# Mixture of experts on tiles of two 64-row halves, biases as a product with the gates, and a last tile in two parts

## The chip, the cores and the metric

The kernel runs on one core of one Trainium2 chip. A core has five instruction queues that run at the same time and meet through semaphores: TensorE (PE in the profile; PEld is its weight load), VectorE (DVE), ScalarE (ACT), GpSimd (POOL) and SyncE (SP, which here only issues transfers and loads registers). The metric is the time of one execution on the device, in microseconds (us); lower is better. The kernel before took 1554.63 us, the median of 5 runs (1551.43 to 1561.74).

## What is computed

A stack of four blocks on `x` (16 batches of 112 tokens, 256 features, float32). Each block adds gated cross attention to a context of 375 tokens a batch and then a gated feed-forward part. Layers 0 and 1 have a mixture of eight experts as feed-forward part, with two experts for each token; layer 2 has eight experts with a fixed share of the tokens; layer 3 has a gated unit whose operands are all quantised to 4 bits in blocks of 16.

```python
x = x + tanh(g_xattn[l]) * attention_l(layernorm(x), ctx)      # l = 0..3; layer 1 has a mask
x = x + tanh(g_ffn[l]) * ffn_l(layernorm(x))

# ffn of layer 0 (layer 1: the softmax over the two chosen experts alone)
gates = softmax(x @ gate_w.T + gate_b)
top_gates, top_idx = top_k(gates, 2)
expert_out[e] = x @ expert_w[e].T + expert_b[e]
out = sum over the two chosen experts of top_gate * expert_out

# ffn of layer 3; w_gate and w_up are 704 x 256, w_down is 256 x 704
h = silu(fp4(x) @ fp4(w_gate).T) * (fp4(x) @ fp4(w_up).T)
out = fp4(h) @ fp4(w_down).T
```

The inputs have biases for the experts of both mixtures that are not zero.

## The kernel before

Everything stays in SBUF as far as it fits: `x` as four tiles of four batches (a group `g`, 448 tokens), the transposed context of all batches. PSUM is two pools: `wide` (line 62), three tiles of two banks, and `bank` (line 66), two tiles of one bank. Whoever asks for a fourth wide tile waits until the first has been read.

The order of instructions on PE, ACT, DVE and POOL is written out by hand, in the order of the Python code. Only SP's order is the scheduler's own: it places each transfer and each register load by its estimate of when it can go.

- **Layers 0 to 2, attention.** `unmasked` (L712) writes the order for layers 0 and 2, one batch after the other; `with_mask` (L839) for layer 1, in 64 units of four heads. A unit in layer 1 computes the scores of the next unit on PE (L449), takes them through the mask on DVE (L615), finds maxima (L632), takes exponentials on ACT (L635), turns them on PE (L647, copied at L651), and multiplies with the values (L664). In layers 0 and 2 the scores are computed twice, once for the maxima (L449, L465) and once transposed (L500, with the maxima added by L512) for the exponentials (L521), and weighted at L536.
- **The mixtures run in the gaps.** Between the attention's pieces the hand-written order calls `fill()` (L1256). A call takes one step of each of three lines of generators: `route` (L975), `products` (L1138) and `combine` (L1207). Each line works on one group of one layer at a time, and passes it to the next line. There are eight jobs: layers 0 and 1, four groups each. The mixture of layer 0 so lies beside the end of layer 0's attention and the start of layer 1's; that of layer 1 beside layer 1's and layer 2's.
- **`route`** normalises the group's rows (`xn`), computes gates, chooses two experts for each token (`top2`), and finds for each token and chosen expert a row in a table in DRAM (`rows_in`): each expert has a region of 512 rows, and a token's place in it is its rank among the tokens of that expert (`pp`, a product with a triangle). Eight indirect transfers from POOL (L1101) write the rows there. A small table (L1124 to L1129) gives, for each of 14 tiles of 128 rows, the expert and the first row.
- **`products`** goes through the 14 tiles (`NS`). Each tile reads its expert and its first row from the table into registers of SP (L1148, L1155), loads 128 rows (`xg`), the expert's weights (`w`, 256 KB) and its bias to all partitions (`wb`), multiplies (L1186), transposes the next tile's rows (L1196), and copies both results out of one PSUM tile with one ACT copy (L1198). POOL adds the bias (L1169); the result goes to `rows_out` in DRAM at the tile's row (L1166). A job has 19 steps.
- **`combine`** gathers for each token its two rows (L1216, POOL's queue) and adds them to `x`, each times its gate (L1224).
- **Tail.** The quantised down weights of layer 3 are made in steps beside layer 0's attention (`weights_down`, L1482) and kept in SBUF (`wd`, L1801). `last_block` (L1547) runs attention and feed-forward of layer 3: 14 tiles of 128 tokens, each with gate and up products (L1688), `silu` (L1698), product (L1700), quantisation over several steps (`fp4`, L1403 to L1422), six transpositions (L1712), a copy (L1716), the down product (L1722) and an add (L1732). Their steps are interleaved with the next tiles' steps; the last tile has nothing behind it.

At the start, SP issues the first weights and contexts one after the other, and ACT issues three small loads. The tables' 4992 rows (`ROWS`) are cleared in DRAM four times during layer 0 (L967).

Of the kernel before, what the change touches and what calls it, by code (L numbers as in the profile page):

```python
# [12 lines left out]
F32 = mybir.dt.float32  # L13
I32 = mybir.dt.int32
U32 = mybir.dt.uint32
# [17 lines left out]
WB, XB = 3, 3  # L33
CAP = 512
NS = (2 * GS + E * (P - 1)) // P
ROWS = E * CAP + (NS - 2 * GS // P) * P
# [11 lines left out]
def tile_gated_xattn_stack(ctx: ExitStack, tc: tile.TileContext, a: dict, out: bass.AP):  # L48
# [29 lines left out]
    def load_ctx(b):  # L78
        nc.gpsimd.memset(ctxZ[b][:, :, T:], 0.0)
        nc.sync.dma_start(ctxT[b], a["ctx"][:, :, b * T : (b + 1) * T])  # L80

    w_first = {n: wpool.tile([P, 2, D], F32, tag=n, name=f"w_0_{n}") for n in ("wq", "wk", "wv", "wo")}
    for n in ("wk", 0, "wv", "x", "wq", 1, "wo"):
        if n == "x":
            load_x(0)
        elif n in w_first:
            nc.sync.dma_start(w_first[n], a[f"L0_xattn_{n}"])
        else:
            load_ctx(n)
# [7 lines left out]
    hmask = const.tile([P, 2], F32, tag="hmask", name="hmask")  # L97
    nc.scalar.dma_start(hmask, a["head_mask"])
# [16 lines left out]

    region = ramp(S, E, CAP, "region")[:, None, :].to_broadcast([S, G, E])
    filled = ramp(E, CAP // P, P, "filled")
    slots = ramp(E, NS, 1, "slots")
    slot_rows = ramp(1, NS, P, "slot_rows")
    coef = const.tile([E, 2], F32, tag="coef", name="coef")  # L120
    nc.gpsimd.memset(coef, 1.0)
    graw = const.tile([P, 8], F32, tag="graw", name="graw")
    nc.scalar.dma_start(graw[:, 0:4], a["g_xattn"].partition_broadcast(P))
    nc.scalar.dma_start(graw[:, 4:8], a["g_ffn"].partition_broadcast(P))
# [131 lines left out]
    def attention(pool, layer, w):  # L256
# [455 lines left out]
        def unmasked(nxt, block):  # L712
# [21 lines left out]
            for b in range(B):  # L734
# [44 lines left out]
                if b == 1:  # L779
                    if layer == 0:  # L780
                        prepare()
                        said["side"] = weights_down(wd)
# [145 lines left out]
    def top2(v, nm):  # L928

        picked = []  # L930
        for i in range(2):
            m = small.tile([S, G], F32, tag="tm", name=f"tm_{nm}_{i}", bufs=2)
            nc.vector.tensor_reduce(m, v, AX.X, ALU.max)
            eq = small.tile([S, G, E], F32, tag="teq", name=f"teq_{nm}_{i}", bufs=2)
# [7 lines left out]
            if i == 0:  # L942
                v2 = small.tile([S, G, E], F32, tag="tv", name=f"tv_{nm}", bufs=2)
# [17 lines left out]
    gate_weights = {}  # L961
# [9 lines left out]
    def mixture_weights(layer):  # L971
        L = f"L{layer}_ffn_"
        gate_weights[layer] = load(wpool, L + "gate_w", [P, 2, E], "gw"), load_row(L + "gate_b", "gb", E)

    def route(layer, g, out):  # L975
# [41 lines left out]
        lg = small.tile([S, G, E], F32, tag="lg", name=f"lg_{nm}", bufs=2)  # L1017
# [27 lines left out]
        picked, keep = chosen  # L1045
        keepb = small.tile([S, G * E], BF16, tag="keepb", name=f"keepb_{nm}", bufs=2)
        nc.vector.tensor_copy(keepb, keep.rearrange("s g e -> s (g e)"))
        nc.vector.tensor_scalar(gt, gt, gate[:S, 4 + layer : 5 + layer], None, ALU.mult)
# [31 lines left out]
        over = small.tile([E, CAP // P], F32, tag="over", name=f"over_{nm}", bufs=2)  # L1080
        nc.vector.tensor_scalar(over, filled, cnt, None, ALU.is_lt)
        tiles_of = small.tile([E, 1], F32, tag="ntiles", name=f"ntiles_{nm}", bufs=2)
        nc.vector.tensor_reduce(tiles_of, over, AX.X, ALU.add)
        place = small.tile([S, G, E], F32, tag="place", name=f"place_{nm}", bufs=2)
        nc.vector.tensor_tensor(place, pp[:S, : G * E].rearrange("s (g e) -> s g e", e=E), region, ALU.add)
# [6 lines left out]
        nc.vector.tensor_copy(index, at)  # L1092
        out.update(picks=picks, index=index)
# [14 lines left out]

        copy_out(0, 0)
        yield  # L1110
        copy_out(0, 1)
        yield
        pe = wide(f"pends_{nm}")[:, 0, :]
        nc.tensor.matmul(pe[:E, 0:1], tri8, tiles_of, start=True, stop=True)
        ends = small.tile([E, 1], F32, tag="ends", name=f"ends_{nm}", bufs=2)
        nc.vector.tensor_copy(ends, pe[:E, 0:1])
        behind = small.tile([E, NS], F32, tag="behind", name=f"behind_{nm}", bufs=2)
        nc.vector.tensor_scalar(behind, slots, ends, None, ALU.is_ge)
        nc.vector.tensor_scalar(coef[:, 1:2], tiles_of, -float(P), float(CAP), ALU.mult, ALU.add)
        copy_out(1, 0)  # L1120
        yield
        pt = wide(f"ptab_{nm}")[:, 0, :]
        for i in range(2):
            nc.tensor.matmul(  # L1124
# [769 lines left out]
```

## Time and profile before

| what | value |
|---|---|
| median of 5 runs | 1554.63 us (1551.43 to 1561.74) |
| the profiled execution, its own time | 1555.78 us |
| its span, first to last instruction | 1554.1 us |
| mean granted TensorE clock | 0.973 |
| L1186, products of the mixtures | 118.8 us busy |
| L1196, transpositions of their rows | 40.5 us busy |
| L1198, ACT copies of both | 63.2 us busy |
| L1169, POOL adds of the biases | 81.6 us busy |
| transfers w_m, 112 of 256 KB | 3.6 us to landing |
| transfers wb_m, 112 of 128 KB | 3.6 us to landing |

A busy time is the time in which at least one instruction of the group ran. A float32 matmul shows as two records, each a pass with its own weight load. Several matmuls that use different rows or columns of the array can run at the same time; then the records overlap, and the mean time times the count is more than the busy time. "Idle before" is the engine's idle time just ahead of the group's instructions, and the arrow names what ended it. Rows for a stretch (`A:B`) give its length and then the busy time and the number of records of PE, PEld, DVE, ACT and POOL, the granted clock, the share of the DMA engines and GB/s. A line of the order of time has start, length, engine, line, what is written from what, the number of merged instructions, and in brackets the idle time before.

### The profile page before, as it was taken

How to read it: one execution, taken by the hardware profiler on the slowest of the kernel's cores; microseconds unless marked ns; L12 is line 12 of the kernel's file. 1: busy time of each engine (PE TensorE's matmuls, PEld its weight loads, DVE VectorE, ACT ScalarE, POOL GpSimd, SP SyncE). 2: the span in 40 equal slices, each digit the busy share in tenths (PEclk: the TensorE clock that was granted, in tenths of full speed). 3: DMA queues.
4: the chain of work that ended last, by engine and by line, in shares of the span. 5: the costliest groups of instructions: out<-in, count | busy, mean ns of one | idle time of the engine just before them, and what ended most of it. 6: DMA issues, size and time to landing. Idle time of an engine off the chain costs nothing.

```text
span 1554.1 us, 34714 instructions
## 1 busy us (share of the span) xinstructions
PE 1458.9 (94%) x13340; PEld 1020.4 (66%) x13340; DVE 961.7 (62%) x1831; ACT 766.3 (49%) x1535; POOL 556.7 (36%) x1004
## 2 busy tenths in 40 slices
PE   7999999989999999998998999999999999999997
PEld 4665656657566676675766565666556788777775
DVE  3566645665678687777776456536555434376786
ACT  2444434435566666666665354444444433446532
POOL 2212123433464446426425245231201234242342
PEclk8999899999999999999998999999999999999999
DMA  9870025334154353442532332420000552110000
GB/s 252 273 264 5 1 59 150 88 117 144 57 142 125 88 158 107 126 130 78 162 92 87 107 103 87 150 82 14 9 2 15 209 167 99 33 41 26 27 20 21
DMA packets 129422, 152.15 MB, mean 98 GB/s; under 512 B 13912, under 2 KB 120488, under 8 KB 127208
## 3 DMA queue, kind: packets, MB, share of 16 engines
q1 hardware_dynamic: 122680, 135.24, 29.2%
q0 software_dynamic: 6144, 14.69, 3.1%
q8 instruction: 105, 1.72, 0.5%
q14 instruction: 61, 0.50, 0.1%
q10 hardware_dynamic: 432, 0.01, 0.0%
HBM read 103.75 MB, written 44.30 MB: 95 GB/s over the span
## 4 chain that ended last, share of the span: by engine, by line
PE 40%; DVE 6%; ACT 3%; POOL 1%; issue 1%; SPq 1%; DMA 1%; POOLq 0%; ACTq 0%; DVEq 0%
PE py_f L1346 4%; PE ps L449 4%; PE ph L1330 3%; PE pgu_h L1688 3%; PE pv L406 3%; PE pt L500 3%; PE po L536 3%; PE pm_m L1186 2%; PE pk L231 2%; PE py L1722 2%; DVE nm L465 1%; PE pz L1612 1%; PE ps L1588 1%; PE py L577 1%; PE pe L647 1%
## 5 line engine op out<-in xcount | busy, mean ns | idle before, releaser
L465 DVE TENSOR_REDUCE nm<-ps 112x2 f32<-112x750 f32 x256 | 230.0, 934 | 197.9 <-PE ps L449 194.9
L449 PE MATMUL ps<-kT,qm 32*112 32x375 f32 (+1 forms) x1536 | 214.4, 526 | 19.0 <-ACT ex L521 13.2
L521 ACT ACTIVATE ex<-pt 125x896 f32<-125x896 f32 x192 | 165.6, 914 | 79.9 <-PE pt L512 79.8
L635 ACT ACTIVATE sm<-sm,nmax 112x375 f32<-112x375 f32 x256 | 152.4, 600 | 4.3 <-DVE nmax L632 3.9
L615 DVE SCALAR_TENSOR_TENSOR sm<-ps,up 112x752 f32<-112x752 f32 x128 | 114.5, 934 | 58.4 <-PE ps L449 57.8
L647 PEld LDWEIGHTS pe<-ident,sm 112*125 112x125 f32 x768 | 103.5, 195 | 51.3 <-ACT sm L635 38.0
L647 PE MATMUL pe<-ident,sm 112*125 112x112 f32 x768 | 115.6, 284 | 22.7 <-ACT sm L635 14.2
L1186 PE MATMUL pm_m<-w_m,xy_m 128*128 128x256 f32 x416 | 118.8, 409 | 14.8 <-DMA w_m<-in_L_ffn_expert_w_dram 7.7
L500 PE MATMUL pt<-qm,kT 32*125 32x224 f32 x1536 | 119.8, 392 | 5.7 <-DVE nm L465 4.4
L1169 POOL TENSOR_TENSOR xy_m<-xy_m,wb_m 128x256 f32<-128x256 f32 x112 | 81.6, 730 | 116.1 <-ACT xy_m L1198 115.4
L449 PEld LDWEIGHTS ps<-kT,qm 32*112 32x112 f32 x1536 | 72.1, 171 | 76.5 <-ACT ex L521 31.9
L1198 ACT COPY xy_m<-pm_m 128x512 f32<-128x512 f32 x112 | 63.2, 565 | 108.2 <-PE pm_m L1196 66.2
L632 DVE TENSOR_REDUCE nmax<-sm 112x2 f32<-112x752 f32 x128 | 113.0, 924 | 0.0
L1186 PEld LDWEIGHTS pm_m<-w_m,xy_m 128*128 128x128 f32 x416 | 72.8, 193 | 55.5 <-ACT eT L651 16.2
L473 POOL CAST mparts<-nm 112x16 bf16<-112x16 f32 x32 | 9.1, 284 | 273.5 <-DVE nm L465 273.5
L406 PE MATMUL pv<-w_L_xattn_wv,ctx 128*125 128x256 f32 x384 | 101.2, 402 | 0.1
L500 PEld LDWEIGHTS pt<-qm,kT 32*125 32x125 f32 x1536 | 77.0, 191 | 35.0 <-issue 14.2
L536 PE MATMUL po<-ex,vpad 125*32 125x112 f32 x3072 | 99.0, 272 | 0.9 <-DVE vals L558 0.6
L231 PE MATMUL pk<-ctx,w_L_xattn_wk 128*128 128x376 f32 (+1 forms) x256 | 93.1, 498 | 0.9 <-ACT qm L392 0.9
L651 ACT COPY eT<-pe 125x672 f32<-125x672 f32 x96 | 68.8, 717 | 50.1 <-PE pe L647 47.5
L536 PEld LDWEIGHTS po<-ex,vpad 125*32 125x32 f32 x3072 | 74.9, 114 | 28.2 <-issue 21.2
L406 PEld LDWEIGHTS pv<-w_L_xattn_wv,ctx 128*125 128x125 f32 x384 | 69.5, 194 | 22.9 <-issue 9.5
(330 smaller groups left out, 2744.8 us busy)
## 6 DMA issues: line engine op xcount, KB each, us to landing
w_m<-in_L_ffn_expert_w_dram SPq DMA_DIRECT2D x112, 256.0 KB, 3.6
w<-in_L_ffn_w_dram SPq DMA_DIRECT2D x16, 1024.0 KB, 4.8
xg_m<-rows_in SPq DMA_DIRECT2D x112, 128.0 KB, 2.4
wb_m<-in_L_ffn_expert_b_dram SPq DMA_DIRECT2D x112, 128.0 KB, 3.6
rows_out<-xy_m SPq DMA_DIRECT2D x112, 128.0 KB, 2.7
rows_in<-zero SPq DMA_DIRECT2D x2, 4992.0 KB
rows_out<-zero SPq DMA_DIRECT2D x2, 4992.0 KB
ctx<-in_ctx_dram SPq DMA_DIRECT2D x16, 375.0 KB, 10.5
```

The lines of the kernel that those rows point to most:

```text
L231: nc.tensor.matmul(ps[:, :n], w[:, k, c * P : (c + 1) * P], rhs[:, k, :n], start=(k == 0), stop=(k == 1))
L406: nc.tensor.matmul(pv[:TC, i * D : (i + 1) * D], rhs_of(b)[:, k, t * TC : (t + 1) * TC], w["wv"][:, k, :], start=(k == 0), stop=(k == 1),)
L449: nc.tensor.matmul(ps[:S, i, :TK], qms[g][rows, c, p, j * S : (j + 1) * S], kTs[b][rows, c, :TK], start=True, stop=True,)
L465: nc.vector.tensor_reduce(nms[b][:, cp, 2 * h : 2 * h + 2], ps[:S, :, :T], AX.X, ALU.max, negate=True)
L500: nc.tensor.matmul(pairs[r // 2][:TC, r % 2, q * 2 * S : (q + 1) * 2 * S], kTs[b][rows, c, t * TC : (t + 1) * TC], qms[g][rows, c, :, j * ...
L521: nc.scalar.activation(e[:, 2 * h : 2 * h + 2].rearrange("t r q p s -> t r (q p s)"), pairs[h][:TC, :, : 4 * S], AF.Exp)
L536: nc.tensor.matmul(po[32 * r : 32 * r + 32, (2 * c + p) * S : (2 * c + p + 1) * S], vp[:, t, 4 * c + r, p : p + 2, :], e[:, r, q, p, :], s ...
L615: nc.vector.scalar_tensor_tensor(sm[:, 2 * h : 2 * h + 2, :], ps[:S, :, :TK], -100.0, uppers[b][:, None, :].to_broadcast([S, 2, TK]), ALU.max,
L632: nc.vector.tensor_reduce(part, sm[:, 2 * h : 2 * h + 2, :], AX.X, ALU.max, negate=True)
L635: nc.scalar.activation(sm[:, i, :T], sm[:, i, :T], AF.Exp, bias=nmax[:, i : i + 1], accum_out=rss[b][:, head : head + 1])
L647: nc.tensor.transpose(pt[:TC, i, t * S : (t + 1) * S], sm[:, 2 * h + i, t * TC : (t + 1) * TC], ident[:S, :S])
L1186: nc.tensor.matmul(pt[:, 1, :D], xgT[:, k * P : (k + 1) * P], w[:, k * D : (k + 1) * D], start=(k == 0), stop=(k == 1),)
```

## The change

- **Tiles of two halves.** A tile of 128 rows is now two halves of 64 rows, each with an expert of its own. An expert's tokens fill whole halves, not whole tiles; a group needs 11 tiles (22 halves) in place of 14. The product is four matmuls, two of 64 output rows for each half of the contraction.
- **Rows in order of the halves.** An expert's rows start behind all halves of the experts before it (`front`, a small product in `route`). A tile's rows are therefore at a fixed place: `xg` and the stores need no register any more. The tables have 1408 rows, not 4992, and only the experts of the 22 halves are read into registers.
- **Biases.** `route` adds the biases to `x` itself: the gates (zero for experts that were not chosen, times the layer's gate) are transposed and multiplied with the table of biases, two batches in a step (`peb`), and DVE adds the result to `x`. The bias loads for each tile and POOL's adds go.
- **Steps.** `products` has 18 steps a job, three of them empty behind every fourth tile; `route` has as many as before, with the pieces in another order.
- **Last tile in two parts.** Layer 3's last tile is worked in parts of 384 and 320 columns (`hidden_in_parts`, `down_in_parts`).
- **Down weights through DRAM.** They are written to `kept` in DRAM in layer 0 and loaded again at the start of the tail, ahead of its masks.
- **Start.** The first context goes through ACT's queue, ahead of its small loads. Some small tiles have one buffer instead of two.

```diff
-WB, XB = 3, 3
-CAP = 512
-NS = (2 * GS + E * (P - 1)) // P
-ROWS = E * CAP + (NS - 2 * GS // P) * P
+WB, XB = 6, 4
+HT = 64
+NS = ((2 * GS + E * (HT - 1)) // HT + 1) // 2
+NH = 2 * NS
+ROWS = NS * P
...
-            load_ctx(n)
+            load_ctx(n, nc.sync if n else nc.scalar)
...
+        eb = expert_bias[layer] = wpool.tile([P, D], F32, tag="eb", name=f"eb_{layer}")
+        for j in range(G):
+            nc.sync.dma_start(eb[32 * j : 32 * j + E, :], a[L + "expert_b"])
...
+        nc.vector.tensor_scalar(gt, gt, gate[:S, 4 + layer : 5 + layer], None, ALU.mult)
+        nc.vector.tensor_tensor(gpad[:, :, :E], gt, keep, ALU.mult)
...
-        nc.vector.tensor_tensor(place, pp[:S, : G * E].rearrange("s (g e) -> s g e", e=E), region, ALU.add)
+        nc.vector.tensor_copy(place.rearrange("s g e -> s (g e)"), pp[:S, : G * E])
+        yield
+        pe = wide(f"pends_{nm}")[:, 0, :]
+        nc.tensor.matmul(
+            pe[:S, :E], halves_of.to_broadcast([E, S]), front, start=True, stop=True, skip_group_check=True
+        )
+        nc.tensor.matmul(pe[:E, 64:65], tri8, halves_of, start=True, stop=True, skip_group_check=True)
+        nc.vector.tensor_tensor(place, place, pe[:S, None, :E].to_broadcast([S, G, E]), ALU.add)
...
+        pt = wide(f"ptab_{nm}")
+        nc.tensor.matmul(pt[:1, 0, :NH], one, behind, start=True, stop=True)
+        nc.tensor.transpose(pt[:, 1, :S], gpad.rearrange("s g e -> s (g e)"), ident[:S, :S])
...
+        nc.scalar.copy(gT, pt[:, 1, :S])
...
+        for half in range(2):
+            pb = wide(f"peb_{nm}_{half}")
+            for i in range(2):
+                j = 2 * i + half
+                nc.tensor.matmul(
+                    pb[:S, i, :D],
+                    gT[32 * j : 32 * j + E, :],
+                    expert_bias[layer][32 * j : 32 * j + E, :],
+                    start=True,
+                    stop=True,
+                )
+            xs = x[g][:, half::2, :]
+            nc.vector.tensor_tensor(xs, pb[:S, :, :D], xs, ALU.add)
...
-            r = regs[s] = nc.sync.value_load(table[0:1, NS + s : NS + s + 1], min_val=0, max_val=ROWS - P)
             xgs[s] = moe.tile([P, D], F32, tag="xg", name=f"xg_{nm}_{s}", bufs=XB)
-            nc.sync.dma_start(xgs[s], rows_in[g][bass.ds(r, P), :])
+            nc.sync.dma_start(xgs[s], rows_in[g][s * P : (s + 1) * P, :])
...
-            wb = moe.tile([P, D], F32, tag="wb", name=f"wb_{nm}_{s}", bufs=WB + 1)
-            nc.sync.dma_start(wb, a[L + "expert_b"][bass.ds(e, 1), :].partition_broadcast(P))
...
+            for n in range(2 * s, 2 * s + 2):
+                e = nc.sync.value_load(table[0:1, n : n + 1], min_val=0, max_val=E - 1)
+                w = moe.tile([P, 2 * D], F32, tag="w", name=f"w_{nm}_{n}", bufs=WB)
+                nc.sync.dma_start(w.rearrange("p (k d) -> p k d", k=2), a[L + "expert_w"][:, :, bass.ds(e * D, D)])
...
-                nc.gpsimd.tensor_tensor(y, y, wb, ALU.add)
...
+                    for h, w in enumerate(both):
+                        nc.tensor.matmul(
+                            pt[h * HT : (h + 1) * HT, 1, :D],
+                            xgT[:, k * P + h * HT : k * P + (h + 1) * HT],
+                            w[:, k * D : (k + 1) * D],
+                            start=(k == 0),
+                            stop=(k == 1),
+                        )
...
+            if s % 4 == 3:
+                yield
...
+                nc.sync.dma_start(
+                    kept[:, 3 * h : 3 * h + 3, k * P : (k + 1) * P], part.rearrange("p (c d) -> p c d", d=P)
                 )
...
+        PARTS = ((0, 3 * P), (3 * P, FI - 3 * P))
+
+        def hidden_in_parts(b):
+
+            u, i = divmod(b, 2)
+            pgu = []
+            for n, (o, m) in enumerate(PARTS):
+                ps = wide(f"pgu_h3_{b}_{n}")
+                for s in range(2):
+                    for k in range(2):
+                        nc.tensor.matmul(
+                            ps[:, s, :m], fTs[u][:, 2 * k + i, :], wT[s][:, k, o : o + m], start=(k == 0), stop=(k == 1)
+                        )
+                pgu.append(ps)
+            yield
...
+        def down_in_parts(b):
+            q, py = hq[b % 3], wide(f"py_3_{b}")
+            hT = pool.tile([P, 2, 3 * P], F32, tag="hT", name=f"hT3_{b}")
+            for n in range(2):
+                pt = bank(f"pht_{b}_{n}")
+                for c in range(3):
+                    nc.tensor.transpose(pt[:, c * P : (c + 1) * P], q[:, (3 * n + c) * P : (3 * n + c + 1) * P], ident)
+                nc.scalar.copy(hT[:, n, :], pt[:, : 3 * P])
+                for c in range(3):
+                    nc.tensor.matmul(
+                        py[:, 0, :D],
+                        hT[:, n, c * P : (c + 1) * P],
+                        wd[:, 3 * n + c, :],
+                        start=(n + c == 0),
+                        stop=(n + c == 3),
+                    )
...
-    wd = const.tile([P, NHC, D], F32, tag="wd", name="wd")
+    kept = dram.tile([P, NHC, D], F32, tag="kept", name="kept")
...
+                wd = pool.tile([P, NHC, D], F32, tag="wd", name="wd", bufs=1)
+                nc.sync.dma_start(wd, kept)
```

## The prediction

> **What bounds the kernel now.** I read the page's first two parts, then the costliest groups, busy times by stage, and single stretches of the order of time. Busy times first:
>
> ```profile
> PE 1458.9 (94%) x13340; PEld 1020.4 (66%) x13340; DVE 961.7 (62%) x1831; ACT 766.3 (49%) x1535; POOL 556.7 (36%) x1004
> ```
>
> TensorE is busy nearly all the time, so what it no longer does should come off the span, unless another engine already sets the pace there. The mixtures' products lie between 200 and 1065 us. Groups that matter (busy us, mean ns | idle before):
>
> ```profile
> L1186 PE MATMUL pm_m<-w_m,xy_m 128*128 128x256 f32 x416 | 118.8, 409 | 14.8 <-DMA w_m<-in_L_ffn_expert_w_dram 7.7
> L1169 POOL TENSOR_TENSOR xy_m<-xy_m,wb_m 128x256 f32<-128x256 f32 x112 | 81.6, 730 | 116.1 <-ACT xy_m L1198 115.4
> L1700 DVE TENSOR_TENSOR h_h<-pgu_h,h_h 128x704 f32<-128x704 f32 x14 | 12.4, 887 | 4.6 <-PE pgu_h L1688 4.1 <-ACT h_h L1698 0.5
> L664 PE MATMUL po<-eT,vpad 125*32 125x112 f32 x1536 | 51.6, 267 | 0.5 <-ACT eT L651 0.5
> ```
>
> Two batches of layer 1 (masked) and two of layer 2, as busy time by stretch; the second fence is the same for the tile pm_m alone, six TensorE records a tile (four of products, two of transposes):
>
> ```profile
> 744.00:770.10 26.10, 26.00 (x240) 19.29 (x238) 20.86 (x35) 18.47 (x49) 12.17 (x19) 1.00 0.62 165
> 521.60:545.80 24.20, 21.51 (x211) 14.97 (x210) 19.93 (x33) 16.28 (x45) 11.88 (x15) 1.00 0.43 109
> 969.80:995.50 25.70, 23.41 (x259) 16.26 (x260) 11.93 (x18) 11.08 (x19) 4.81 (x11) 1.00 0.55 168
> 1106.40:1126.70 20.30, 19.61 (x232) 12.12 (x235) 11.05 (x16) 8.22 (x14) 3.88 (x9) 0.92 0.01 2
> ```
>
> ```profile
> 744.00:770.10 26.10, 8.09 (x36) 5.75 (x36) 3.44 (x6) 1.00 0.62 165
> 521.60:545.80 24.20, 1.35 (x6) 0.96 (x6) 0.58 (x1) 1.00 0.43 109
> 969.80:995.50 25.70, 6.69 (x31) 5.14 (x32) 2.92 (x5) 1.00 0.55 168
> ```
>
> In layer 1 five tiles more (36 against 6 records) lengthen a batch by only 1.9 us, 0.38 a tile: DVE is busy there for 20 of 24 us, and TensorE waits in the batch that has few tiles. In layer 2, 5.2 tiles add 5.4 us, 1.04 each. A least-squares fit over layer 1's 62 units gives 0.62 a tile. So a tile is worth 1.04 in layers 0 and 2 and 0.38 to 0.62 in layer 1; I take 0.55.
>
> **1. Fewer tiles.** Eleven instead of 14 a group, eight groups: 24 fewer. By the order of instructions 11 of them leave layers 0 and 2 (52 become 41) and 13 leave layer 1 (60 become 47). 11 x 1.04 + 13 x 0.55 = **-18.6 us**. Bounds: 0.38 in layer 1 gives -16.4; 1.22, TensorE's whole price (0.97 of products, 0.22 of transposes), gives -27.3. The ACT copies that go (24 of 565 ns) are in these prices.
>
> **2. Switches of the array's shape.** The two halves of a tile write 64 columns of the array each. From the start times of the single matmul records, a switch between full, 32-row and 32-column shapes costs 93 ns more than streaming: transposes 109 ns apart stand 202 before L664, and 256-column matmuls 216 apart stand 309 before L500. The first pass after a switch is longer too, by 25 ns (32-column weights), 50 (transposes) or 104 (L1186). Each of 88 tiles now pays a switch from product to transposes, 0.14; 25 that came after full-shape work pay one on entry, 0.14; the others save perhaps 0.05, since 64 columns lie between 32 and 128. In all 12.3 + 3.6 - 3.2 = 12.7 us of TensorE. 41 tiles in layers 0 and 2 pay it fully (5.9), 47 in layer 1 at 0.55/1.22 (3.1): **+9.0** (+4 to +13).
>
> The products themselves should cost the same: L664 gives 1536 records of 267 ns in 51.6 us, so column groups run side by side, weight loads included. The Trainium skill, "TensorE: Matmul & The Clock Gate", Part 3, says that a weight load overlaps a running matmul only when their row groups differ; the halves share all rows, so by it the second half would follow the first. By the rule the time would come to some 1600 us, by L664 to the sum below; L664, whose four groups also share their rows, speaks against it.
>
> **3. Biases.** Per group four 8-row matmuls in two steps, with two VectorE adds on 512 columns. Four 32-row matmuls of 376 columns take 0.93 us from start to the next instruction (604.13 to 605.06), a switch included; at 256 columns 0.63, with the second switch 0.70. An add: 512 elements lie between 484 ns (256, L1353) and 887 (704, L1700): 0.70. In layers 0 and 2 six steps pay TensorE's price, 4.2. In layer 1 ten steps: a product tile behind one more PSUM tile waits there for VectorE,
>
> ```profile
> 503.75 0.24 PE L1124 MATMUL ptab_m<-behind_m,coef 8*1 8x14 f32 x4
> 504.82 1.13 PE L1186 MATMUL pm_m<-w_m,xy_m 128*128 128x256 f32 x4 [0.82 <-DVE sm L615]
> ```
>
> so between 0.3 (0.55/1.22 of 0.70) and 1.1 (0.24 + 0.82); I take 0.5, nearer the low end, because VectorE has finished its two score operations by the time the step's own matmuls end: 5.0. **+9.2** (+7 to +15). What leaves, 112 POOL adds of 730 ns and as many bias loads, lies beside other work; TensorE waits for POOL's mparts 2.2 us in all, so **-1** (0 to -3).
>
> **4. Routing.** Place becomes copy and add, and one transposition of the gates, its ACT copy (0.35) and a scaling are new; a row of the table goes. Per group about 0.16 us of TensorE and 0.4 of VectorE, half of it visible: **+2** (0 to +5). The number of steps stays.
>
> **5. SP's queue.** The scheduler gathers register loads of the table in front of transfers. In layer 0 they hold SP from 320.8 to 333.9 (23 loads at 0.57), and the next weights come late:
>
> ```profile
> 320.34 0.46 SPq L1159 DMA_DIRECT2D wb_m<-in_L_ffn_expert_b_dram  x1
> 334.13 0.34 SPq L1150 DMA_DIRECT2D xg_m<-rows_in  x1
> 334.66 0.59 SPq L1157 DMA_DIRECT2D w_m<-in_L_ffn_expert_w_dram  x1
> ...
> 338.10 2.04 PE L1186 MATMUL pm_m<-w_m,xy_m 128*128 128x256 f32 x4 [5.03 <-DMA w_m<-in_L_ffn_expert_w_dram]
> ```
>
> The tile after the stall takes 2.04 instead of 1.13 us: the granted clock is 0.50 there, which costs 1.7 more. Rows now need no register: 22 loads a group instead of 28, and three tiles' weights are issued ahead of the block of 16 loads (9 us). Tiles there follow each other at some 4 us, so the fourth comes after the weights: **-6.7** (0 to -9.4, the 7.7 of all such waits and the clock). A tile moves 512 KB of weights instead of 384 with biases; the lead stays two tiles, against 3.6 us to landing, so I charge nothing; with one tile of lead it would be the late transfer.
>
> **6. Last tile.** One chain from 1537.16:
>
> ```profile
> 1544.75 1.43 POOLq L1890
> 1546.22 0.89 PE pht L1712 x6
> 1547.19 0.81 ACT hT L1716
> 1548.04 2.87 PE py L1722 x12
> ```
>
> In parts of 384 and 320, with operations scaled by width, quantising the second part overlaps the first's POOL product, and the first three transposes, copy and products run under the second's. Followed operation by operation the final add comes at 1549, not 1550.9: **-2.1** (-1 to -3).
>
> **7. Ends.** ctx 0 on ACT's queue lets x leave SP 0.7 us sooner, into a filled DMA: **-0.5** (0 to -1). At 1334 the down weights' load (768 KB, some 3 us at the page's 273 GB/s) now precedes the masks on SP, which have 3 to 4 us of slack until the first scores: **+0.5** (0 to +1.5).
>
> **Sum:** -18.6 + 9.0 + 9.2 - 1 + 2 - 6.7 - 2.1 - 0.5 + 0.5 = -8.2. The profiled execution took 1555.78 (span 1554.1, 1.7 around it), 1.15 above the median of 1554.63; less 8.2 it would take 1547.6, and the median **1546 us**, 0.5% faster. 0.5% (7.8 us) is also about what a measurement can tell from no change.
>
> **Rivals.**
> - *More gain (1535):* layer 1 gives TensorE's whole 1.22 a tile, 8.7 more, and all waits for weights go, 2.7 more. For it: POOL stands 115 us behind ACT at L1169 with other work queued. Against: the 0.38 above.
> - *The stall only moves (1553):* blocks of 14 to 16 loads remain, one tile waits as long as before elsewhere: 6.7 back. For it: in later groups the rows are issued behind the block.
> - *Slower (1564):* the wide PSUM tiles are three, and the biases' tile is freed only by VectorE's add, which queues behind two score operations of 0.93 us. If each of the sixteen steps then holds TensorE for the whole round, it costs 0.24 + 0.82 of the fence in part 3 and the add's 0.70, 1.8 us, in layer 1, and twice 0.70 in layers 0 and 2: 13 and 4.2 more than I took, -8.2 + 17.2 = +9. It decides, by 0.5%, at 1.6 us a step. Against it: most waits of TensorE in layer 1 are for ACT (0.33 to 0.96 us), not for VectorE.
> - *Halves one after the other (1600):* four more passes of 216 ns, 0.86 us a tile: 41 full and 47 at 0.45 are 53.5, with -8.2 a loss of 45. Against it: L664. The rule named in part 2 would have it so.
>
> **How the numbers follow.** Forecast 0.40, falling either side of -0.5% (0.25 faster, 0.15 same); more gain 0.20; stall moved 0.15; held by VectorE 0.13; halves in turn 0.05; unseen 0.07 (0.05 faster, 0.02 slower). Faster 0.50, same 0.30, slower 0.20. The range takes in the first four cases with their bounds: 1531 to 1566.
>
> **What would show it.** In the changed profile: 704 product records in pairs a few ns apart, tiles of 1.37 us; 32-row matmuls for peb of about 0.6; batches of layer 1 between 23 and 29 us; no 5 us wait for w_m near 333; the last add some 12 us after the last gate and up product, not 14. It is wrong if product records stand one after another, if idle time before masked scores or peb goes to DVE, or if a load block stands ahead of first weights.

## The result, and the profile after

The changed kernel takes 1542.64 us (median of 30 runs, 1534.59 to 1557.29), the kernel before 1555.09 in the same comparison (56 runs): ratio 0.9934, 95% interval 0.9917 to 0.9951. (This is the first comparison; the expectations below call it the blind result.) Forecast were 1546 us and 0.5% faster. The profiled execution took 1544.3 us (span 1542.4), so the span is 11.7 us shorter than the one the prediction was made from. That is the result on the chips of this comparison. On another chip the same change makes the kernel 2.4% slower, and on a third chip two versions that differ little from it are slower by as much; eight of the experiments ran on these two, and most of what follows is about that.

The first line of the profile's page of the changed kernel, busy time by engine:

```profile
PE 1454.0 (94%) x13620; PEld 978.6 (63%) x13620; DVE 966.8 (63%) x1854; ACT 756.8 (49%) x1522; POOL 480.9 (31%) x897
```

TensorE is busy 4.9 us less, POOL 75.8 us less, VectorE 5.1 more. The groups that answer to those shown of before (busy us, mean ns | idle before):

```profile
L1212 PE MATMUL pm_m<-w_m,xy_m 128*64 128x256 f32 x640 | 88.2, 397 | 6.8 <-DVE sm L622 2.9 <-DVE nm L472 1.6 <-ACT qm L399 1.3
...
L1149 PE MATMUL peb_m<-eb,gT_m 8*112 8x256 f32 x64 | 13.3, 480 | 0.1
L1157 DVE TENSOR_TENSOR x<-peb_m,x 112x512 f32<-112x512 f32 x16 | 11.0, 686 | 9.0 <-PE peb_m L1149 9.0
```

640 records of 397 ns in 88.2 us: the two halves of a tile run at the same time. Their single records start 7 ns apart, and the next pair 210 to 260 ns later. (All 704 that the change issues have a record, eight for each of the 88 tiles; 64 of them, those of the first tile of each job, stand in the trace under another tile name, and the line leaves them out.) The waits for `w_m`, 7.7 us before, are gone from the first line. The products of the biases hardly wait (0.1 us).

The place of the 5.03 us wait, in order of time (start, us; SPq is the issue of transfers):

```profile
308.84 1.94 SPq L1188 DMA_DIRECT2D w_m<-in_L_ffn_expert_w_dram  x2
...
312.27 1.96 SPq L1188 DMA_DIRECT2D w_m<-in_L_ffn_expert_w_dram  x2
...
323.75 0.33 SPq L1179 DMA_DIRECT2D xg_m<-rows_in  x1
324.20 1.08 PE L1212 MATMUL pm_m<-w_m,xy_m_-1_3791 128*64 128x256 f32 x8
325.21 0.44 PE L1222 MATMUL pm_m<-ident,xg_m 128*128 128x128 f32 x2
325.31 1.38 SPq L1188 DMA_DIRECT2D w_m<-in_L_ffn_expert_w_dram  x2
...
328.68 1.08 PE L1212 MATMUL pm_m<-w_m,xy_m 128*64 128x256 f32 x8
```

SP still issues nothing for 9.5 us (16 register loads, from 314.2 to 323.7), but the weights of the first three tiles were issued ahead of that block (the first pair at 294), and the tiles at 324 and 328 wait for nothing.

How far the changed kernel is ahead, at the batches' output adds (L580/L587 in layers 0 and 2) of the two profiles, with the time that the trace's clock records give at half speed in each stretch:

| up to (us of before) | ahead by, us | half speed, before / after, us |
|---|---|---|
| 212 | 8.3 | 34.1 / 10.2 |
| 332 | 4.3 | 0 / 13.7 |
| 400, end of layer 0 | 11.8 | 3.4 / 0 |
| 932, first batch of layer 2 | 8.8 | 23.9 / 27.3 |
| 1222, last batch of layer 2 | 10.7 | 20.5 / 17.1 |
| end of the span | 11.7 | 3.4 / 5.9 |

The first row is a surprise: 8 us are gained before a tile of the mixtures has run. There the change does nothing on TensorE; it clears 1408 DRAM rows in place of 4992 and starts a context elsewhere. The clearest step lies in the third row: 6.9 us between the adds at 332 and 365, where the wait was. Just ahead of it the changed kernel loses almost as much: it is 11.0 us ahead at the add of 288 and 4.3 at that of 332, and in between it has its 13.7 us at half speed. So one pair of profiles shows where the wait went, but not by itself what that is worth in the end.

### The profile page after: what moved, and what is told of

Read it like the earlier page. It is cut to its first block, busy times and chain, and to the rows that moved or that the text cites. A ratio compares the mean times of both kernels' runs of the same rounds, so it can differ in the third digit from the quotient of the medians.

```text
span 1542.4 us, 34417 instructions
## 1 busy us (share of the span) xinstructions
PE 1454.0 (94%) x13620; PEld 978.6 (63%) x13620; DVE 966.8 (63%) x1854; ACT 756.8 (49%) x1522; POOL 480.9 (31%) x897
## 4 chain that ended last, share of the span: by engine, by line
PE 41%; DVE 6%; ACT 3%; issue 1%; POOL 0%; ACTq 0%; DVEq 0%; POOLq 0%
PE py_f L1373 4%; PE ps L456 3%; PE ph L1357 3%; PE pgu_h L1717 3%; PE pv L413 3%; PE pt L507 3%; PE po L543 3%; PE pk L238 2%; PE py L1809 2%; DVE nm L472 2%; PE pm_m L1212 2%; PE pe L654 1%; PE pz L1641 1%; PE ps L1617 1%; PE py L584 1%; ACT ex L528 1%
## 5 line engine op out<-in xcount | busy, mean ns | idle before, releaser
L456 PE MATMUL ps<-kT,qm 32*112 32x375 f32 (+1 forms) x1536 | 215.5, 524 | 19.8 <-ACT ex L528 13.1
L528 ACT ACTIVATE ex<-pt 125x896 f32<-125x896 f32 x192 | 165.7, 914 | 76.3 <-PE pt L519 76.3
L507 PE MATMUL pt<-qm,kT 32*125 32x224 f32 x1536 | 117.6, 382 | 6.5 <-DVE nm L472 5.9
L639 DVE TENSOR_REDUCE nmax<-sm 112x2 f32<-112x752 f32 x128 | 113.1, 924 | 0.0
L413 PE MATMUL pv<-w_L_xattn_wv,ctx 128*125 128x256 f32 x384 | 101.5, 402 | 0.1
L238 PE MATMUL pk<-ctx,w_L_xattn_wk 128*128 128x376 f32 (+1 forms) x256 | 94.6, 504 | 0.9 <-ACT qm L399 0.9
L1212 PE MATMUL pm_m<-w_m,xy_m 128*64 128x256 f32 x640 | 88.2, 397 | 6.8 <-DVE sm L622 2.9
L1224 ACT COPY xy_m<-pm_m 128x512 f32<-128x512 f32 (+1 forms) x88 | 49.4, 561 | 91.2 <-PE pm_m L1222 43.2
L413 PEld LDWEIGHTS pv<-w_L_xattn_wv,ctx 128*125 128x125 f32 x384 | 69.5, 194 | 23.1 <-issue 9.7
L423 ACT COPY vpad<-pv 125x256 f32<-125x256 f32 x96 | 32.7, 375 | 103.8 <-PE pv L413 103.8
L587 DVE SCALAR_TENSOR_TENSOR x<-py,gate,x 112x256 f32<-112x256 f32 x32 | 15.5, 484 | 98.5 <-PE py L584 98.5
```

Source lines behind the costliest of these rows:

```text
L238: nc.tensor.matmul(ps[:, :n], w[:, k, c * P : (c + 1) * P], rhs[:, k, :n], start=(k == 0), stop=(k == 1))
L413: nc.tensor.matmul(pv[:TC, i * D : (i + 1) * D], rhs_of(b)[:, k, t * TC : (t + 1) * TC], w["wv"][:, k, :], start=(k == 0), stop=(k == 1),)
L456: nc.tensor.matmul(ps[:S, i, :TK], qms[g][rows, c, p, j * S : (j + 1) * S], kTs[b][rows, c, :TK], start=True, stop=True,)
L507: nc.tensor.matmul(pairs[r // 2][:TC, r % 2, q * 2 * S : (q + 1) * 2 * S], kTs[b][rows, c, t * TC : (t + 1) * TC], qms[g][rows, c, :, j * ...
L528: nc.scalar.activation(e[:, 2 * h : 2 * h + 2].rearrange("t r q p s -> t r (q p s)"), pairs[h][:TC, :, : 4 * S], AF.Exp)
L639: nc.vector.tensor_reduce(part, sm[:, 2 * h : 2 * h + 2, :], AX.X, ALU.max, negate=True)
```

## The experiments

Theory A for the early gain: the smaller clears. Rival B: chance of the clock in one profile. The first four kernels were run on one chip.

**The kernel before once more** (no edit).

> The kernel before, unchanged, to see how its granted clock and its first 200 us vary from run to run. In the profile of the changed kernel some 7 of the 11.7 us of span are already gained at 200 us, before any tile runs. Theory A (the four clears of the DRAM rows shrink from 4992 to 1408 rows each and the early DMA traffic with them): the mean granted clock of these runs stays below that of the changed kernel's runs (about 0.977), near 0.973, and the long dip after 30 us (13.7 us) is here again. Theory B (chance of the clock in the one profile): the mean clock over these runs is the changed kernel's, 0.977, and the first 200 us scatter by 5 us or more. The time itself: 1555, ratio 1.000.

It took 1591.0 us beside a kernel before of 1593.02 (0.9983, 0.9951 to 1.0015): a chip on which this kernel takes 38 us more than in the first comparison. Its profile has no half-speed stretch at 30 us, and its third batch is weighted (L547) at 72.6 us, not at 76.3 as in the first profile; in the changed kernel that was 72.1. So the same kernel scatters by about 4 us at this point: this speaks for B.

**Clears of 4992 rows in the changed kernel.**

```diff
-        [dram.tile([ROWS, D], F32, tag=f"{n}{i}", ...
+        [dram.tile([39 * P, D], F32, tag=f"{n}{i}", ...
-            ... zero[:, None, :].to_broadcast([P, ROWS // P, D])
+            ... zero[:, None, :].to_broadcast([P, 39, D])
```

> The changed kernel with row buffers of 4992 rows, all cleared, as before; the order of work on TensorE is the same. Theory A: most of the early gain is lost, so 1547 to 1549, ratio about 0.996 to 0.998. Theory B: 1542 to 1544, ratio 0.993 to 0.994, within 1 us of the changed kernel, since the clears lie beside TensorE's work.

**The last tile whole.**

```diff
-            hid = quant[f] = (hidden_in_parts if f == NTL - 1 else hidden)(f) if 0 <= f < NTL else none
+            hid = quant[f] = hidden(f) if 0 <= f < NTL else none
-            if 0 <= f - 2 < NTL - 1:
+            if 0 <= f - 2 < NTL:
-            added = (down_in_parts if f - 2 == NTL - 1 else down)(f - 2) ...
+            added = down(f - 2) ...
```

> The changed kernel with the last tile whole, as before. By the prediction's sixth term 2.1 us slower (1 to 3): 1544 to 1545.5, ratio 0.9940 to 0.9954, and the last addition ends 14 us after the last gate and up product instead of 12. By the landmarks of the two profiles (10.7 us gained when the last product of the gates and ups of the tail begins, 11.7 at the end) about 1.0 us: 1543.6.

**No bias steps.** The matmuls into `peb` and the additions to `x` are taken out.

> The changed kernel without the sixteen bias steps (32 products of the gates and 16 additions left out; the output lacks the experts' biases, the gates' transposition stays). By the prediction's third term it is 9.2 us faster (7 to 15): 1533, ratio 0.987 to 0.988. Rival, that the steps fill waits of TensorE in layer 1: only the 6 of layers 0 and 2 count with 0.7 each, 4 us: 1538 to 1539, ratio 0.990 to 0.991.

Measured: 1629.63 us with the large clears (1.0243, 1.0203 to 1.0282), 1632.16 with the whole last tile (1.0235, 1.0197 to 1.0272), 1609.42 without biases (1.0105, 1.0068 to 1.0141). The first two agree within their intervals of some 6 us either way, and up to the last add ahead of the first long stop their profiles agree too (186.5 us with the large clears, 187.1 with the small ones). So the clears cost nothing that can be seen, and theory A falls. All three missed every number of mine by 70 us or more. Their traces show why: TensorE stands still for up to 13 us at a time; such a stop is called a hold from here on. Theory H came from this: a train of POOL's indirect transfers (the scatters L1123 and gathers L1243) holds TensorE up on this chip. The next four ran on a second chip.

**The changed kernel once more** (no edit).

> The changed kernel, unchanged. In the first four runs the kernel before took 1593 instead of 1555 and three versions of the changed kernel took 1609 to 1632, 1.0 to 2.4% more than it; in their traces TensorE's semaphore does not move for 3 to 13 us at a time (308.3 to 321.4 in the run with a whole last tile, with 522 packets of POOL's indirect transfers inside) and moves again within 0.1 us of the last such packet or some 0.6 us behind it. Theory H (trains of indirect transfers hold up TensorE on that chip and not on the one of the blind result): beside a kernel before of 1593 this takes 1625 to 1632, ratio 1.020 to 1.025, with holds of 8 to 13 us in layers 0 to 2; beside a kernel before of 1555 it takes 1543 (0.993) and has no such holds. Rival (what was changed in those three versions made them slow): 1582 beside 1593, ratio 0.993, on either chip.

1619.48 us beside 1582.63 for the kernel before: ratio 1.0244 (1.0212 to 1.0276). So the three edits were not the reason; the changed kernel as it is is slow there too. One stretch of this run in order of time:

```profile
985.00 0.69 PE L1149 MATMUL peb_m<-eb,gT_m 8*112 8x256 f32 x4
...
986.53 0.90 PE L456 MATMUL ps<-kT,qm 32*112 32x375 f32 x8
...
987.00 0.94 POOL L1123 DMA_INDIRECT rows_in<-xn_m,index_m  x1 [0.21 <-issue]
...
988.66 0.21 PE L492 MATMUL pm<-identb,mparts 112*128 112x112 bf16 x1 [0.41 <-issue]
...
995.83 0.95 POOL L1243 DMA_INDIRECT yg_m<-rows_out,index_m  x1 [0.30 <-issue]
...
998.71 1.78 DVE L472 TENSOR_REDUCE nm<-ps 112x2 f32<-112x750 f32 x2 [12.27 <-remote]
998.88 0.53 ACT L496 COPY mr<-pm 128x448 bf16<-128x448 bf16 x1 [12.73 <-remote]
```

And the same instructions in the changed kernel's profile of the first comparison:

```profile
932.24 0.69 PE L1149 MATMUL peb_m<-eb,gT_m 8*112 8x256 f32 x4
...
933.76 0.90 PE L456 MATMUL ps<-kT,qm 32*112 32x375 f32 x8
...
934.51 0.94 POOL L1123 DMA_INDIRECT rows_in<-xn_m,index_m  x1 [0.21 <-issue]
...
934.69 1.79 DVE L472 TENSOR_REDUCE nm<-ps 112x2 f32<-112x750 f32 x2 [1.03 <-PE ps L456]
...
935.43 0.53 ACT L496 COPY mr<-pm 128x448 bf16<-128x448 bf16 x1 [2.04 <-PE pm L492]
```

VectorE reads the scores 12.2 us after their matmuls began in the held run and 0.9 us after in the other. POOL issues the same nine transfers in both, 0.94 to 0.97 us each. By stretch (PE, PEld, DVE, ACT and POOL busy, granted clock, DMA share, GB/s), first the held run, then the other:

```profile
985.80:998.60 12.80, 2.58 (x48) 1.48 (x40) 0.63 (x1) 0.35 (x1) 10.70 (x16) 0.77 0.42 129
```

```profile
933.20:944.30 11.10, 9.88 (x148) 6.18 (x137) 5.13 (x7) 4.73 (x8) 8.96 (x14) 1.00 0.48 147
```

The chain of waits of the held run has no releaser for it, and the DMA part counts what ran meanwhile, 432 packets of POOL's queue (q0):

```profile
986.43 12.25 another core or an unknown queue
```

```profile
q0 software_dynamic: 432, 1.03, 26.8%
q1 hardware_dynamic: 650, 0.62, 15.2%
```

In the trace, TensorE's semaphore does not move from 985.72 to 998.68; the last of these packets starts 0.49 us before it moves again. Most other holds end within 0.6 us of the start of the last packet of a train (308.32 to 321.42 in the run with the whole last tile: 14 ns). The instructions on TensorE have their records in the meantime; what stays away is the signal that they are done. From within the longest holds on the clock records show half speed for 10 to 27 us. The Trainium skill, "TensorE: Matmul & The Clock Gate", Part 1, has the clock halved after an idle window of some 3.4 us; the trace agrees in the length, its half-speed pieces are multiples of 3.41 us. What that makes of the whole run, on the profile's pages of the kernel before (on the first of these chips) and of the changed kernel (on the second):

```profile
PE 1475.5 (93%) x13340; PEld 1028.8 (65%) x13340; DVE 961.2 (60%) x1831; ACT 766.4 (48%) x1535; POOL 556.5 (35%) x1004
```

```profile
PE 1487.1 (92%) x13620; PEld 997.2 (62%) x13620; DVE 966.6 (60%) x1854; ACT 757.4 (47%) x1522; POOL 480.3 (30%) x897
```

TensorE's idle time (span less busy) is 117.6 us in a span of 1593.1 there, against 95.2 in the first profile of the kernel before; for the changed kernel 126.7 of 1613.8 against 88.4. Its busy time grows by 16.6 and 33.1, with 37 and 88 us more at half speed. So the kernel before has holds too: its span is 39 us longer than in the first profile, that of the changed one 71 us. These are two chips; on the second alone the kernel before takes 1582.63 us, 28 more than in the first comparison, and the changed one 77 more. The time in holds does not show this difference. On the first chip the kernel before has 17 holds of over 3.2 us with 77 us in sum, the changed kernel with the whole last tile 11 with 80. The single holds are longer (longest 9.7 and 13.1 us), and half speed takes 123 and 198 us.

Why longer? POOL has no additions between its transfers any more, and the scatters of a group lie in five steps, not six. In the first profile of the kernel before, q0's packets form 92 stretches without a pause of 0.6 us, the longest 4.4 us; in that of the changed kernel 52, the longest 11.3.

**POOL's additions put back** (zeros instead of the bias; the store follows a tile later).

```diff
+            if adds:
+                s, y = adds.pop(0)
+                nc.gpsimd.tensor_tensor(y, y, nil, ALU.add)
+                stores.append((s, y))
...
-                stores.append((s, xy[:, 1, :]))
+                adds.append((s, xy[:, 1, :]))
```

> The changed kernel with an addition of zeros on POOL for each tile, where the addition of the bias stood (88 of 0.73 us); the store follows it, one tile later. By the prediction's accounting POOL's additions lie beside other work: +1 us (0 to 3). Theory H: on a chip with holds the additions stand between POOL's transfers and cut the trains, so it gets faster by 5 us or more against the changed kernel; without holds +1 (0 to 3).

1610.32 us, ratio 1.0169 (1.0137 to 1.0201): 9 us less than the changed kernel, as H asked. But its profile does not show the reason H gave: there are 18 holds of over 3.2 us, 85 us in sum, against 13 with 78 us. Nor do the additions cut the trains: q0's packets form 58 stretches, the longest 11.2 us, against 57 and 10.0 without them. Why it is faster is open.

**Whole products.** Two products of 128 columns a tile; the second expert of a tile is left out of the first half of the contraction and the first out of the second.

```diff
-                    for h, w in enumerate(both):
-                        nc.tensor.matmul(
-                            pt[h * HT : (h + 1) * HT, 1, :D],
-                            xgT[:, k * P + h * HT : k * P + (h + 1) * HT],
-                            w[:, k * D : (k + 1) * D],
+                    nc.tensor.matmul(
+                        pt[:, 1, :D],
+                        xgT[:, k * P : (k + 1) * P],
+                        both[k][:, k * D : (k + 1) * D],
```

> The changed kernel with two products of 128 columns a tile instead of four of 64 (each tile uses one expert for the first half of the input and another for the second, so the output is wrong; all six transfers stay). By the prediction's second term the switches go: 9.0 us faster (4 to 13), 0.58% less than the changed kernel beside it. Rival, that the switches hide behind waits: within 2 us of it. In the trace a tile should take some 1.13 us on TensorE instead of 1.37.

1609.72 us, ratio 1.0171 (1.0151 to 1.0192): 9.8 us less than the changed kernel beside it. Its holds are about as long (11 with 74 us), but its profile has 135 us at half speed, the changed kernel's 162, so not all of the 9.8 us need be the switches. The groups of its tile:

```profile
L1211 PE MATMUL pm_m<-w_m,xy_m 128*128 128x256 f32 x320 | 90.3, 405 | 7.1 <-DVE sm L622 2.9 <-DVE nm L472 1.7 <-ACT qm L399 1.3
...
L1221 PE MATMUL pm_m<-ident,xg_m 128*128 128x128 f32 x160 | 30.8, 274 | 0.0
```

Half as many records take the same busy time, 90.3 against 88.2 us: two halves cost one pass. What the halves add are the switches. From the first product of a tile to the instruction behind its transposes it is 1.29 us with halves and 1.19 whole (median of 80 tiles each). On entry the halves cost 0.03 to 0.09 us more for 25 of these tiles (behind L238, L413, L1014, L1020 and L1135), and nothing for the others.

**Fourteen tiles.**

```diff
-NS = ((2 * GS + E * (HT - 1)) // HT + 1) // 2
+NS = 14
```

> The changed kernel with 14 tiles a group instead of 11 (the last ones hold nothing that is used): 24 more tiles of 1.37 us. By the first two terms (1.04 in layers 0 and 2 and 0.55 in layer 1, plus the switches of 0.24 and 0.11): 11 x 1.28 + 13 x 0.66 = 23 us slower (18 to 33), 1.5%. Rival, tiles that fill waits of TensorE in layer 1: 14 us, from layers 0 and 2 alone.

1612.27 us, ratio 1.0185 (1.0150 to 1.0221): 7 us less with 24 more tiles, hardly more than the noise of four runs. The expectation failed in sign. Its profile has 6 holds with 25 us, where the changed kernel had 13 with 78, so what the tiles cost is hidden under what the holds give back. Its trains are shorter (70 stretches, the longest 6.2 us), which fits H, but the kernel before had trains as short on the first of these chips (the longest 5.4 us) and 17 holds. The price of a tile stays unmeasured.

Three of the last four kernels take the transfers away, the fourth spreads them. They ran on a chip where the kernel before takes 1554.32 us, as in the first comparison: no holds.

**Without indirect transfers**, in both kernels, and in the changed one without the bias steps as well:

```diff
-            inst = nc.gpsimd.indirect_dma_start(
-                rows_in[g], bass.IndirectOffsetOnAxis(index[:, i, j : j + 1], 0), xn[:, j, :], None
-            )
...
-            for i in range(2):
-                nc.gpsimd.indirect_dma_start(
-                    yg[:, i, :], None, rows_out[g], bass.IndirectOffsetOnAxis(index[:, i, j : j + 1], 0)
-                )
+            nc.gpsimd.memset(yg, 0.0)
```

> The kernel before without POOL's 128 indirect transfers: nothing is scattered to the DRAM rows and nothing gathered from them (a memset stands for each gather), so the mixtures add only zeros; all else runs. Theory H (a train of these transfers holds TensorE up on these chips, and its clock is halved behind the longer holds): some 20 us of waits and as much of clock go, 1545 to 1565 beside a kernel before of 1580 to 1593, ratio 0.975 to 0.985. Rival (the transfers only coincide with the holds): 1575 or more, ratio over 0.992.

> The changed kernel without the 128 indirect transfers, in the same way. Theory H: without them the change is worth what it was in the blind result, so 0.993 of the run of the kernel before without transfers (0.990 to 0.997), some 1540; 75 us less than the changed kernel with them. Rival (the halves, the biases or the clock make the change slow on these chips): 1.01 or more of that run.

> The changed kernel without the indirect transfers and without the sixteen bias steps (products of the gates and additions). Measures the prediction's third term where nothing holds TensorE: 9.2 us less than without the transfers alone (7 to 15). The run without biases among holds gave some 21 us less than its neighbours; if that is the steps' own price, it is 21 here too. If only layers 0 and 2 count, 4.

The kernel before takes 1542.65 us without them (ratio 0.9935, 0.9907 to 0.9963), the changed kernel 1541.96 (0.9938, 0.9912 to 0.9965), and without biases 1533.06 (0.9860, 0.9819 to 0.9901). On a chip without holds this says nothing on H. It says something else that I had not asked: the transfers cost the kernel before 11.7 us and the changed kernel, 1542.64 in the first comparison and not run on this chip, about nothing, and without them the change is worth 0.7 us (about ±6). In the kernel before without them the long wait is gone (start, us):

```profile
314.93 0.59 SPq L1151 DMA_DIRECT2D w_m<-in_L_ffn_expert_w_dram  x1
...
329.45 0.35 SPq L1144 DMA_DIRECT2D xg_m<-rows_in  x1
329.99 0.59 SPq L1151 DMA_DIRECT2D w_m<-in_L_ffn_expert_w_dram  x1
...
330.11 1.13 PE L1180 MATMUL pm_m<-w_m,xy_m 128*128 128x256 f32 x4
...
334.49 1.13 PE L1180 MATMUL pm_m<-w_m,xy_m 128*128 128x256 f32 x4
```

The same issue of the second tile's weights in the profile of the kernel before:

```profile
319.58 0.58 SPq L1157 DMA_DIRECT2D w_m<-in_L_ffn_expert_w_dram  x1
```

SP's block of register loads is as long as before and has two tiles' weights ahead of it as before, but all of it lies 4.7 us earlier, the second tile's weights at 314.93 and not at 319.58: in the kernel before, SP waits 5.2 us (308.8 to 314.0) ahead of them for the scatters, until it may load rows. So the third tile's weights are issued at 329.99 and not at 334.66, and its products at 334.49 wait for nothing. It gains 5.9 us between the adds at 332 and 365; the changed kernel gained 6.9 there. Of the rest of the 11.7 us, 3.2 come in the profiles behind the add at 1109, where no mixture runs any more, with four half-speed pieces of the clock against two.

**Transfers spread out**: one scatter in each of eight steps, one gather a step.

```diff
-        copy_out(0, 1)
-        copy_out(1, 0)
+        copy_out(1, 0)
...
-        for i in range(2):
-            copy_out(3, i)
-        yield
+        for j, i in ((2, 1), (3, 0), (3, 1)):
+            copy_out(j, i)
+            yield
```

> The changed kernel with its indirect transfers spread out: one scatter a step instead of up to two (eight steps instead of five) and one gather a step instead of two. Its output is the reference's. Theory H: the trains get shorter, no hold of 12 us is left, and it is 10 to 40 us faster than the changed kernel on the same kind of chip: ratio to the kernel before between 0.998 and 1.018, not 1.024. Rival: 1.022 to 1.027 as before.

1546.41 us, ratio 0.9956 (0.9929 to 0.9984), no better than the changed kernel in the first comparison (0.9934). Both theories had asked for a ratio of 0.998 or more, on a chip with holds. Its trains are shorter, 91 stretches, the longest 7.7 us. Whether that helps on a chip with holds was not tried.

## Why the prediction was right, and what it did not see

**The sum.** -8.2 us against a ratio that makes -10.3 (0.66% of 1555); the medians lie 12.5 apart. At one granted clock, 0.977, straight lines through the single runs give 1543.9 us (32 runs of after) and 1552.0 (24 of before, on the last chip): 8.1 apart. The mean clock of these runs is alike, 0.977 and 0.976, so as far as the last chip's runs can stand for those of the first comparison, whose clocks of the kernel before are not on record, the gain is no gift of the clock. The single profiles have such gifts: the 8.3 us ahead at 212 us are mostly chance of the clock, and two profiles of kernels that agree up to there (the last chip's two changed kernels without transfers) stand 8.9 us apart at 178. That the sum fits is in part luck: the terms for the tiles (-18.6 us, its largest) and the routing (+2) were not measured by themselves, and errors that cancel would not show.

**1 and 2, tiles and switches.** A tile takes 1.29 us, and in some places 0.03 to 0.09 more on entry; forecast were 1.37; the switch from products to transposes was forecast at 0.14 and makes a tile 0.10 longer. Removing the switches gave 9.8 us on a held chip, forecast 9.0 (4 to 13), with the doubt about the clock that is told there. The halves run side by side, as L664 had it. The rule named in the prediction, the Trainium skill, "TensorE: Matmul & The Clock Gate", Part 3, would, as it was read there, have made 1600 us; the trace disagrees: starts 7 ns apart on shared rows. The price of a tile, 1.04 and 0.55, was not settled. In layer 1 a fit over 15 batches gives 0.3 to 0.8 us a tile with its switches (each ±0.3 to 0.4), by the instruction at which a batch is cut, which cannot tell it from 0.66. The batches of layer 1 (first maxima to first maxima, L639) take 24 to 34 us, not 23 to 29, and 28.2 in the mean (before 28.0): tiles, switches and biases cancel, as forecast.

**3, biases.** Forecast 9.2, measured 8.9 (1541.96 less 1533.06, without holds; about ±7). The add took 686 ns, forecast 700. On the held chip the same removal gave some 21 us; why more is open.

**4, routing.** Not measured alone. Terms 1 to 4, 6 and 7 together were -1.5, and without transfers, where term 5 is gone from both, it is -0.7 (about ±6).

**5, the stall.** Forecast -6.7, measured -6.9 and, by the other way of removing it, -5.9. The prediction gave the right reason, weights behind a block of loads. It did not say that a wait for the scatters had put the block so late. Within the noise (about ±6 us) this term carries the whole gain: without transfers, where the stall is gone from both kernels, the other gains and costs cancel, as the sum had them.

**6, last tile.** In the tail of the changed kernel (start, us):

```profile
1523.77 2.64 PE L1747 MATMUL pgu_h<-wT,fT_f 128*128 128x384 f32 x9
...
1533.44 0.55 PE L1783 MATMUL pht<-ident,hq 128*128 128x128 f32 x3
...
1535.95 0.49 PE L1783 MATMUL pht<-ident,hq 128*128 128x128 f32 x3
...
1537.01 1.56 PE L1786 MATMUL py<-wd,hT 128*128 128x256 f32 x6 [0.57 <-ACT hT L1784]
1538.61 0.48 DVE L1821 SCALAR_TENSOR_TENSOR xt<-py,gate,xt 128x256 f32<-128x256 f32 x1 [4.49 <-PE py L1786]
```

From the end of the last gate and up product (1526.41) to the final add it is 12.2 us, before 13.9 (1537.05 to 1550.93): -1.7, forecast -2.1. Only 1.0 reaches the end of the span, because the output's transfer ends 3.3 us behind the add, not 2.7. The second profiles of both kernels give 12.2 and 13.9 again. In the runs with a whole last tile nothing of this could be told at 1632 us; the stretch takes 16.7 us in their profile, with 6.8 us at half speed in it.

**7, ends.** The first scores start 0.8 us earlier (21.20 and not 22.01; forecast 0.5). The down weights' load costs nothing: the lead over the kernel before is 10.7 us on both sides of it.

**The rivals.** Of "held by VectorE" nothing is left: L1149 waits 0.1 us, and behind the additions of the biases TensorE waits 0.2 us in all, for a weight load. The stall did not move. "More gain" (1535) is 8 us too low.

**What was missing.** No step and no rival looked at how POOL's transfers follow each other. I costed the additions that leave POOL at -1 us because they lie beside other work, and did not ask what they separate. In the profile of before next to nothing waited for it (2.2 us); on the chip of `after_again` something on that side is worth 47 us, more than four times the gain (ratio 1.0244 instead of 0.9934). Shown: on the two chips the long holds lie inside the trains, single holds are longer in the changed kernel, and it loses more. Argued only: that the transfers are the cause, and that the removed additions and the tighter steps make it worse; POOL's additions put back helped by 9 us without fewer holds or shorter trains, and the runs without transfers met a chip without holds. Open: what TensorE waits for in the hardware, and what sets these chips apart.

## What to carry to other kernels

Two half tiles with different weights can share a pass of the array, and the price is the change of shape around them: here 0.10 us a tile of 1.19, and up to 0.09 more behind some of the work ahead. Look at what stands ahead of a late transfer in its queue, and then at what put it there; here one such block was worth 6 to 7 us, most of the gain. Before you tighten a train of indirect transfers or take away the work between them, time the change on more than one chip: a result of -0.7% with a narrow interval became +2.4% on the next.

## What of the hardware was not expected

- On two of the chips TensorE's semaphore did not move for 3 to 13 us during trains of POOL's indirect transfers, with its matmuls already started by their records, and mostly moved again within 0.6 us of the last packet; the same instructions ran through elsewhere (2.58 of 12.8 us busy against 9.88 of 11.1).
- Matmuls of 64 columns on all rows start 7 ns apart and cost one pass (88.2 us for 640 records of 397 ns); leaving that shape costs 100 ns (310 in place of 210 to the next start), and the first transpose behind it 56 more (165, not 109).
- Two profiles can differ by 8.9 us in their first 178 us through the granted clock: 20.5 us at half speed in one (none_no_bias), none in the other (after_none), in pieces that are multiples of 3.41 us.
